# Splitting three of the seven products a second time in units 2 to 4 of an adjacency-attention kernel

## Chip, cores and metric

The kernel runs on one core of one Trainium2 chip. The metric is the device time of one execution in microseconds (us), the median over runs; lower is better. Engines are named as in the profile: PE (TensorE matmul), PEld (its weight loads), DVE (VectorE), ACT (ScalarE), POOL (GpSimd), SP (the queue that issues most loads).

## The reference, cut to what matters

x is 4096 x 512 and adj is 4096 x 4096, all float32. Two layers run after one another; the change touches only the last product of the second one.

```python
def _L1_gnn_ref(x, adj, weight, bias, node_w, edge_w):
    node_att = softmax(x @ node_w, axis=0)
    h = x @ edge_w
    e = h @ h.T
    e = where(adj > 0, e, NEG_BIG)
    edge_att = softmax(e, axis=1)
    combined_att = node_att * edge_att
    support = x @ weight
    output = adj * combined_att @ support
    return output + bias
...
x = layernorm(x + _L0_gnn_ref(x, adj, L0_gnn_weight))
x = layernorm(x + _L1_gnn_ref(x, adj, L1_gnn_weight, ...))
```

The kernel computes adj * combined_att times x first and multiplies by `weight` afterwards, row block by row block.

## The kernel before, in words

**Stages.** Up to about 870 us the first layer runs, then h is made, then the scores e with their row minima and sums are written to DRAM. From 1081.8 us to the end, the stage that matters here, the *aggregate*, multiplies the weights by x. It consists of 16 units, `blocks` (L1256), each an `Aggregate(g, r)`: g is one of four pairs of 512-wide column groups of the result (groups g and g+4), r one of four pairs of 512-deep blocks that are summed over. Units 1 to 4 are the first column pair (g = 0; r = 0, 1, 2, 3), units 5 to 8 the second, and so on. A unit's number n in the code is one less: `n` = 0 to 3 is the first pair.

**A unit.** It is a 2 x 2 block product done by seven products instead of eight. Its right operands are four square pieces of 512 x 512 weights, `self.q`, in buffers of 8 KB per partition, and three combinations `t2, t3, t4` of them; its left operands lie ready in DRAM, `lop_d[r][:, m]` for m = 0 to 6 (512 deep, 256 wide). While unit n is multiplied, the other engines make the right operands of unit n+1. `steps` (L858) lists this work with the fraction of the unit at which each item is traced: load scores and adjacency (POOL queue), `shift` (L823, DVE), `exp` and `clip` (L826 and L829, ACT), `weigh` (L835, DVE), `combine` (L848 to L856, DVE). There are twelve DVE operations of 128 x 2048 in it. `extra`, two more such buffers, is taken when n reaches 4.

**A product.** In the plain form product m is two objects `Sums(unit, m, h)`, h = 0 and 1, each with a PSUM bank of its own, four matmuls of 128x128 by 128x512. `in_two(n)` (L1258) says which units use the other form: there the products m in `SPLIT = 6, 4, 3` are themselves done by seven products of half size, in four `Sums` with `ns` = (1, 2), (6,), (0, 5), (3, 4), where `ns` are the numbers of the half-size products in that bank, each two matmuls of 128x128 by 128x256. `in_two` is true for n = 4 to 14: every column pair but the first, and not the last unit. `order` (L914) gives the order of the products; in a split unit it is one end, 6, 5, 4, 0, 3, the other end.

**What a split product needs.** Right combinations: `second` (L935; four DVE operations of 128 x 512, L942 to L946), written into `extra[0]` and over the old right operand. Left combinations: `lefts` (L949; four DVE operations of 128 x 256, L955 to L958, in the two `left2` buffers of the pool `rows`, which has four buffers). In this kernel the units of the first pair make them after each plain product m in `SPLIT` has been multiplied, from the left operand that lies in SBUF, and ACT sends them to DRAM (`lop2_d`, L962); the units of the other pairs read them back together with the raw quarters (L1048 to L1052).

**Sums over r.** A bank is copied by ACT to `sums` (or, for ns (0, 5) and (6,), to `extra`) when its product is done (`evict`, L1074) and copied back into a bank before the same product of the next unit (`seed`, L1037). When the fourth unit of a pair is done, the half-size products are put together by `join_inner` (L1098, seven DVE operations of 128 x 256 for each m, L1113), then the seven products by `join` (L1115, 128 x 1024, L1128). `Finish` (L1132) then multiplies by `weight` (L1192, PE) and adds into x (L1203, DVE). It runs off the list `todo` during the next three units.

**What sets the order.** The text of the program gives each engine's stream roughly; the framework's scheduler may move an instruction forward on its engine when it holds it ready. `tc.keep_in_program_order` pins an instruction behind the one traced before it on its engine. PE's products follow `plan`; `seed` runs up to three `Sums` ahead; left operands are loaded by SP into the pool `lopp` (four buffers).

Of the kernel before, what the change touches and what calls it, by code (L numbers as in the profile page):

```python
# [11 lines left out]
F32 = mybir.dt.float32  # L12
# [6 lines left out]
P = 128  # L19
# [4 lines left out]
SHIFT = 1.5 * 2.0**34  # L24
SPLIT = 6, 4, 3
WARM = 12


@with_exitstack
def kernel(  # L30
# [13 lines left out]
    nc = tc.nc  # L44
# [3 lines left out]
    W = 512  # L48
# [605 lines left out]
    class Couple:  # L654
# [9 lines left out]
        def operands(self):  # L664
            A, B, h = self.A, self.B, KD // 2
            if B not in Couple.right:
                r11, r12 = (hT[:, :h, ts(c, W)] for c in (B, B + 1))
                r21, r22 = (hT[:, h:, ts(c, W)] for c in (B, B + 1))
                t1, t2, t3, t4 = (lopp.tile([P, h, W], F32, name="right", tag="lop") for _ in range(4))
                nc.vector.tensor_sub(t1, r12, r11)  # L670
                nc.vector.tensor_sub(t2, r22, t1)
                nc.vector.tensor_sub(t3, r22, r12)
                nc.vector.tensor_sub(t4, r21, t2)
                Couple.right[B] = r11, r21, r22, t4, t1, t2, t3
            low, high = (hT[:, f : f + h, ts(A, W)].rearrange("p k (q u w) -> p k q u w", u=2, w=P) for f in (0, h))
            l11, l21 = (low[:, :, :, u, :] for u in range(2))
            l12, l22 = (high[:, :, :, u, :] for u in range(2))
            Couple.made[0] += 1
            self.sums = None
            if Couple.made[0] % 2:  # L680
                s2, s1, s3, s4 = (rows.tile([P, h, 2, P], F32, name="left", tag="rows") for _ in range(4))
            else:
                self.sums = Uses(1)
                s2, s1, s3, s4 = (
                    self.sums.buf[:, n, :].rearrange("p (k q w) -> p k q w", k=h, w=P) for n in range(4)
                )
            nc.vector.tensor_add(s1, l21, l22)
            nc.vector.tensor_sub(s2, s1, l11)
            nc.vector.tensor_sub(s3, l11, l21)
            nc.vector.tensor_sub(s4, l12, s2)  # L690
            self.left = l11, l12, s4, l22, s1, s2, s3
# [107 lines left out]
    class Aggregate:  # L799
# [2 lines left out]

        def __init__(self, g, r):
            self.g, self.r = g, r

        def load(self, n):
            r, c = self.r + n // 2 * HG, self.g + n % 2 * HG
# [138 lines left out]
            nc.vector.tensor_sub(t4, r21, t2)  # L946
            yield

        def lefts(self, m, lop):  # L949

            (l11, l21), (l12, l22) = [[lop[:, k : k + 2, f : f + P] for f in (0, P)] for k in (0, BG // 2)]
            s = [rows.tile([P, 2, BG // 2, P], F32, name="left2", tag="rows") for _ in range(2)]
            s4, s3, s2, s1 = (x[:, n] for x in s for n in range(2))

            tc.keep_in_program_order(nc.vector.tensor_add(s1, l21, l22))  # L955
            tc.keep_in_program_order(nc.vector.tensor_sub(s2, s1, l11))
            tc.keep_in_program_order(nc.vector.tensor_sub(s3, l11, l21))  # L957
            tc.keep_in_program_order(nc.vector.tensor_sub(s4, l12, s2))  # L958
            to = lop2_d[self.r][:, SPLIT.index(m)]
            yield  # L960
            for n in range(2):
                nc.scalar.dma_start(to[:, ts(n, 2)], s[n])  # L962
# [5 lines left out]
        def main(self, between, two):  # L968
            uses = deque(u for u in plan if u.unit is self)
            whole = sum(u.work for u in uses)  # L970
            halves = (None for m in [u.m for u in uses if u.ns and u.ns[0] == 1] for _ in self.second(m))
            stores = deque()
            past = 0
            while plan and plan[0].unit is self:
                u = plan.popleft()
                u.seed()
                u.multiply()
                evict()
                written.append(u)
                for ahead in list(plan)[:3]:  # L980
                    ahead.seed()
                past += u.work
                if stores:
                    next(stores.popleft(), None)
                if not u.ns:
                    next(halves, None)
                if u.end:
                    free.append(self.right(u.m))
                    if not self.g and u.m in SPLIT:
                        stores.append(self.lefts(u.m, lops["lop"]))  # L990
                        next(stores[0])
                between(past / whole, u.work)
            if stores:
                next(stores.popleft(), None)
# [4 lines left out]

        joins = {0: (0,), 5: (1,), 6: (2,), 4: (3, 4, 5), 3: (6,)}  # L1000

    lops = {}
    kept = deque()
    written = deque()

# [2 lines left out]
    class Sums:  # L1008
# [5 lines left out]
        def __init__(self, unit, m, h=0, more=False, keep=False, ns=None):  # L1014
            self.unit, self.m, self.h, self.more, self.keep, self.ns = unit, m, h, more, keep, ns
            self.work = 2 * len(ns) if ns else 8
            self.begin = ns[0] == 1 if ns else not h
            self.end = ns[0] == 3 if ns else bool(h)
            self.w = W // 2 * len(ns) if ns else W
            self.bank = None  # L1020

        def to(self):

# [2 lines left out]
        def seed(self):  # L1026


            if self.bank is not None or self.more and not kept:
                return  # L1030
            if self.more:
                self.bank = kept.popleft()
                return
            self.bank = banks.popleft()
            if self.unit.r:
                assert self.ns or not any(m == self.m for m, _ in [*inner, *inner_next])
                nc.scalar.copy(self.bank[:, : self.w], self.to())  # L1037
            elif self.w < W:
                nc.vector.memset(self.bank[:, : self.w], 0.0)

        def multiply(self):
            r, m = self.unit.r, self.m
            if self.begin and not self.ns:
                lops["lop"] = lopp.tile([P, BG, HD], F32, name="lop")
                nc.sync.dma_start(lops["lop"], lop_d[r][:, m])
            elif self.begin:
                low, high = (lopp.tile([P, 4, BG // 2, P], F32, name="lop2", tag="lop") for _ in range(2))
                raw, s = lop_d[r][:, m], lop2_d[r][:, SPLIT.index(m)]  # L1048
                nc.sync.dma_start(low[:, :2].rearrange("p n b f -> p (n b) f"), raw[:, :, :P])
                nc.sync.dma_start(low[:, 2:], s[:, :2])  # L1050
                nc.sync.dma_start(high[:, :2], s[:, 2:])
                nc.sync.dma_start(high[:, 2], raw[:, BG // 2 :, P:])  # L1052
                lops["low"], lops["high"] = low, high
            if self.ns:
                products = []
                for k, n in enumerate(self.ns):
                    at = self.lefts[n]
                    lop = lops["high"][:, at - 4] if at > 3 else lops["low"][:, at]
                    products.append((self.bank[:, ts(k, W // 2)], lop, self.unit.halves[n], BG // 2))
            else:  # L1060
                products = [(self.bank, lops["lop"][:, :, ts(self.h, P)], self.unit.right(m), BG)]
            start = not r and self.w == W
            for ps, lop, rop, K in products:
                for k in range(K):
                    nc.tensor.matmul(ps, lop[:, k, :], rop[:, k, :], start=start, stop=(k == K - 1), skip_group_check=True)  # L1065
                    start = False
            if self.keep:
                kept.append(self.bank)

        def evict(self):  # L1070
            u = self.unit
            if not self.keep:
                assert u.r or not self.ns or not any(m == self.m for m, _ in [*inner, *inner_next])
                nc.scalar.copy(self.to(), self.bank[:, : self.w])  # L1074
                banks.append(self.bank)
            if self.end and self.ns and (u.r == HG - 1 or blocks.index(u) == len(blocks) - 2):
                inner_next.extend((self.m, n) for n in range(7))
            if self.end and u.last:
                for done in u.joins.get(self.m, ()):
                    join(u.g, done, nc.vector)  # L1080
# [176 lines left out]

    def in_two(n):  # L1258

        return HG <= n < len(blocks) - 1  # L1260

    def couples(B, *As):
        return [Couple(A, B) for A in As]
# [82 lines left out]
    for n, u in enumerate(blocks):  # L1346
# [5 lines left out]
        if n == 0:  # L1352
            first.extend((0.05, f) for _, f in early_)
            first.extend((0.13 + n // 2 * 0.07, lambda n=n: u.combine(n)) for n in range(4))
        elif n == HG:
            extra.extend(take() for _ in range(2))
        if nxt:
            steps = nxt.steps()
# [81 lines left out]
```

## Time and profile before

| what | value |
|---|---|
| median of 3 runs | 1941.57 us (1939.22 to 1943.59) |
| span of the profiled execution | 1940.4 us, mean granted clock 0.999 |
| unit 1 (n = 0) | 1081.82 to 1131.83 us |
| unit 2 (n = 1) | 1131.83 to 1179.90 us |
| unit 3 (n = 2) | 1179.90 to 1227.97 us |
| unit 4 (n = 3) | 1227.97 to 1277.82 us |
| units 5 to 16 | 1277.82 to 1909 us |

The units' edges are the starts of their first aggregate matmul (line L1065) in the order of time. A float32 matmul of the program is two MATMUL rows in the trace (1094 are issued at L1065, 2188 rows are there); a row is called a *pass* below. A row's duration is longer than the distance to the next row, because passes overlap, so costs on PE are read as distances from start to start. In the answer by stretches, each line gives a stretch in us, its length, and for each engine the busy time with the number of instructions in brackets, then the granted clock, the share of the DMA engines and GB/s.

### The profile page before, as it was taken

To read this page: it belongs to the slowest core of one execution; us is meant where nothing else is said; L and a number is where in the kernel's file an instruction comes from. 1 tells how busy PE (TensorE), PEld (TensorE's weight loads), DVE (VectorE), ACT (ScalarE), POOL (GpSimd) and SP (SyncE) were. 2 spreads that over 40 slices of the span, in tenths; PEclk is the share of its full clock that TensorE was granted. 3 is DMA by queue.
4 is the path that set the end of the run, shared out by engine and by line. 5 is a ranking of instruction groups with operands and counts; after the bars stand their busy time and mean duration, and the time that the engine had idled before them with its cause. 6 is when DMAs were issued, how large, how long until landed. Compare 5 with 4: busy or idle time off the path is not lost.

```text
span 1940.4 us, 20257 instructions
## 1 busy us (share of the span) xinstructions
PE 1918.7 (99%) x6742; PEld 1203.0 (62%) x6742; DVE 1389.6 (72%) x2062; ACT 1022.4 (53%) x1614; POOL 299.5 (15%) x424
## 2 busy tenths in 40 slices
PE   9999999999999999999999999999999999999998
PEld 6888888888644445454555444456666666666655
DVE  7766676676774566567566796687879987798737
ACT  5433333333202567566667566546766576757731
POOL 0122222222341111011112111111111101111100
PEclk9999999999999999999999999999999999999999
DMA  9888888888475478577769998787778787887831
GB/s 311 296 325 310 293 324 308 323 306 293 147 274 213 166 253 320 183 279 254 274 249 336 330 336 296 259 284 248 260 268 290 262 278 254 294 274 265 274 108 44
DMA packets 171751, 517.11 MB, mean 267 GB/s; under 512 B 15872, under 2 KB 41216, under 8 KB 163968
## 3 DMA queue, kind: packets, MB, share of 16 engines
q1 hardware_dynamic: 89472, 226.39, 35.0%
q0 software_dynamic: 66912, 247.49, 34.2%
q10 hardware_dynamic: 15264, 41.95, 5.9%
q8 instruction: 53, 0.87, 0.2%
q14 instruction: 50, 0.41, 0.1%
HBM read 389.94 MB, written 125.83 MB: 266 GB/s over the span
## 4 chain that ended last, share of the span: by engine, by line
PE 76%; DVE 10%; issue 6%; DMA 6%; ACT 1%; POOL 1%; POOLq 0%; DVEq 0%; SPq 0%; ACTq 0%
PE bank L1065 25%; PE seven L702 12%; PE acc L374 11%; PE acc L373 11%; PE pe L633 4%; PE seven L101 4%; PE po L1192 3%; PE pt L603 2%; DMA s_d<-slot 2%; DMA slot<-s_d 2%; DVE lent L835 1%; PE acc L246 1%; PE pw L214 1%; PE pt L333 1%; DVE over L1128 1%
## 5 line engine op out<-in xcount | busy, mean ns | idle before, releaser
L1065 PE MATMUL bank<-lent,lop 128*128 128x512 f32 (+1 forms) x1292 | 424.6, 479 | 0.7 <-issue 0.7
L373 PE MATMUL acc<-xw,hi 128*128 128x512 f32 x960 | 376.4, 392 | 0.0
L374 PE MATMUL acc<-xw,lo 128*128 128x512 f32 x960 | 374.2, 390 | 0.0
L1065 PE MATMUL bank<-slot,lop 128*128 128x512 f32 (+1 forms) x896 | 347.0, 535 | 0.3 <-DVE slot L850 0.3
L1065 PEld LDWEIGHTS bank<-lent,lop 128*128 128x128 f32 x1292 | 245.2, 190 | 155.0 <-issue 133.6
L1065 PEld LDWEIGHTS bank<-slot,lop 128*128 128x128 f32 x896 | 170.0, 190 | 153.4 <-issue 142.3
L363 ACT CAST hi<-at 128x1024 fp32r<-128x1024 f32 x120 | 126.4, 1054 | 203.3 <-PE acc L373 148.4
L365 DVE TENSOR_TENSOR lo<-at,hi 128x1024 fp32r<-128x1024 f32 x120 | 146.9, 1224 | 85.3 <-ACT hi L363 85.3
L374 PEld LDWEIGHTS acc<-xw,lo 128*128 128x128 f32 x960 | 180.3, 188 | 37.0 <-DVE lo L365 0.3
L373 PEld LDWEIGHTS acc<-xw,hi 128*128 128x128 f32 x960 | 180.3, 188 | 36.7
L1074 ACT COPY over<-bank 128x512 f32<-128x512 f32 x200 | 114.9, 581 | 121.3 <-PE bank L1065 109.9
L633 PE MATMUL pe<-hT 128*128 128x512 f32 (+3 forms) x384 | 132.1, 486 | 0.0
L574 ACT ACTIVATE line<-line,nmax_c 128x512 f32<-128x512 f32 x160 | 114.8, 724 | 20.9 <-DVE nmax_c L565 20.8
L565 DVE CUSTOM_DVE_ANT_0 line<-lent,slot 128x512 f32<-128x512 bf16 x144 | 93.1, 689 | 45.2 <-ACT slot L643 22.4
L829 ACT ACTIVATE slot<-slot 128x2048 f32<-128x2048 f32 x40 | 76.5, 1913 | 73.8 <-DMA slot<-in_adj_t_dram 64.7
L823 DVE CUSTOM_DVE_ANT_1 slot<-slot,line 128x2048 f32<-128x2048 f32 x36 | 82.4, 2288 | 32.2 <-DMA slot<-s_d 31.7
L633 PEld LDWEIGHTS pe<-hT 128*128 128x128 f32 x384 | 64.6, 191 | 41.4 <-issue 33.8
L702 PE MATMUL seven<-hT 128*128 128x512 f32 x192 | 89.8, 593 | 0.0
L826 ACT ACTIVATE slot<-slot 128x2048 f32<-128x2048 f32 x36 | 68.9, 1913 | 33.5 <-DVE slot L823 32.5
L1037 ACT COPY bank<-over 128x512 f32<-128x512 f32 x144 | 84.8, 596 | 2.9 <-DVE left L957 0.2
L603 PEld LDWEIGHTS pt<-ident,lent 128*128 128x128 f32 x412 | 51.1, 141 | 55.1 <-issue 40.0
L604 ACT COPY slot<-pt 128x512 f32<-128x512 f32 (+3 forms) x126 | 69.5, 555 | 27.8 <-PE pt L603 24.0
(260 smaller groups left out, 2864.9 us busy)
## 6 DMA issues: line engine op xcount, KB each, us to landing
at<-in_adj_t_dram SPq DMA_DIRECT2D x60, 1024.0 KB, 6.9
slot<-in_adj_t_dram POOLq DMA_DIRECT2D x42, 1024.0 KB, 6.7
lop<-lop_d SPq DMA_DIRECT2D x79, 512.0 KB, 4.7
slot<-s_d POOLq DMA_DIRECT2D x36, 1024.0 KB, 7.5
s_d<-slot POOLq DMA_DIRECT2D x33, 1024.0 KB, 6.9
lent<-s_d POOLq DMA_DIRECT2D x28, 1024.0 KB, 7.9
lop<-lop_d SPq DMA_DIRECT2D x99, 256.0 KB, 4.4
lent<-in_adj_dram SPq DMA_DIRECT2D x48, 512.0 KB, 4.9
```

The costliest lines, as they stand in the source:

```text
L363: nc.scalar.copy(hi, aq)
L365: nc.vector.tensor_sub(lo, aq, hi.bitcast(F32))
L373: nc.tensor.matmul(acc, hi[:, c, :], xw[:, kb, :], start=(kb == 0), stop=False)
L374: nc.tensor.matmul(acc, lo[:, c, :], xw[:, kb, :], start=False, stop=(kb == NB - 1))
L565: nc.vector.tensor_tensor_reduce(line, mask, src, -1.0, HUGE, ALU.add, ALU.min, accum_out=nmax_c[:, b, c : c + 1])
L574: nc.scalar.activation(line, line, AF.Exp, bias=nmax_c[:, b, c : c + 1], scale=-1.0, accum_out=sum_c[:, b, c : c + 1])
L603: nc.tensor.transpose(pt[:, j, :], src[:, ts(j, P)], ident)
L633: nc.tensor.matmul(pe[:, lo * P :], hT[:, k, ts(A * BG + i, P)], hT[:, k, (B * BG + lo) * P : (B + 1) * W], start=(k == 0), stop=(k == KD ...
L702: nc.tensor.matmul(ps, left[m][:, k, q, :], right[m][:, k, :], start=(first and k == 0), stop=(k == KD // 2 - 1), skip_group_check=not first,)
L1037: nc.scalar.copy(self.bank[:, : self.w], self.to())
L1065: nc.tensor.matmul(ps, lop[:, k, :], rop[:, k, :], start=start, stop=(k == K - 1), skip_group_check=True)
L1074: nc.scalar.copy(self.to(), self.bank[:, : self.w])
```

## The change

`in_two` becomes true from n = 1. So products 6, 4 and 3 are split in units 2, 3 and 4 too. The purpose is to have seven half-size products there instead of eight.

In these units a split product doesn't read its left combinations from DRAM: `operands` loads the raw left operand whole, `combine` calls `lefts` up to two `Sums` ahead, and the matmuls read the `left2` buffers and the raw quarters in SBUF. ACT still sends the combinations to DRAM, after the product, for the other column pairs. In all units, the loads of left operands are now traced up to `AHEAD` = 2 `Sums` ahead.

Unit 1 stays plain. Its result for a split m is laid into two of the half-size sums: the half-size sums (1, 2) and (3, 4) of unit 2 are seeded from it, after one DVE subtraction of 128 x 256 for each m, and (0, 5) and (6,) start fresh in unit 2 (a bank that is only half used is zeroed by DVE, L1039). `extra` is taken at n = 1 instead of n = 4. Since the first pair now has half-size sums, `join_inner` runs for it as well, during unit 4.

```diff
+AHEAD = 2
...
-        def lefts(self, m, lop):
+        def lefts(self, m):
+            lop = self.whole[m]
...
+            self.split[m] = l11, l12, s4, l22, s1, s2, s3
...
                 u.seed()
+                u.operands()
+                for ahead in list(plan)[:AHEAD]:
+                    ahead.operands()
                 u.multiply()
...
                     if not self.g and u.m in SPLIT:
-                        stores.append(self.lefts(u.m, lops["lop"]))
-                        next(stores[0])
+                        u.combine()
+                        stores.append(self.stores[u.m])
+                for ahead in list(plan)[:2]:
+                    if ahead.ns and ahead.begin and not self.g:
+                        ahead.combine()
...
+            self.fresh = not unit.r or unit is blocks[1] and ns in ((0, 5), (6,))
...
-            if self.unit.r:
+            if not self.fresh:
...
+        def operands(self):
+
+            u, m = self.unit, self.m
+            if not self.begin or m in u.whole or m in u.split:
+                return
+            raw = lop_d[u.r][:, m]
+            if not self.ns or not u.g:
+                u.whole[m] = lopp.tile([P, BG, HD], F32, name="lop")
+                nc.sync.dma_start(u.whole[m], raw)
+                return
...
+        def combine(self):
+
+            u, m = self.unit, self.m
+            if m not in u.stores:
+                u.stores[m] = u.lefts(m)
+                next(u.stores[m])
...
-            start = not r and self.w == W
+            start = self.fresh and self.w == W
...
+                if u is blocks[0] and self.end and self.m in SPLIT:
+                    upper, lower = (sums[:, 0, self.m, h, W // 2 :] for h in range(2))
+                    nc.vector.tensor_sub(upper, upper, lower)
...
-        return HG <= n < len(blocks) - 1
+        return 0 < n < len(blocks) - 1
...
-        elif n == HG:
+        elif n == 1:
             extra.extend(take() for _ in range(2))
```

## The prediction

> **What bounds the kernel now.** I read the page's first part, then the PE rows in order of time at the end of unit 8, then busy time by stretch with one stretch per unit, then the waits of PE and DVE. The page:
>
> ```profile
> PE 1918.7 (99%) x6742; PEld 1203.0 (62%) x6742; DVE 1389.6 (72%) x2062; ACT 1022.4 (53%) x1614; POOL 299.5 (15%) x424
> ```
>
> PE is the bound of the whole, if its busy time can be trusted. The Trainium skill ("Perfetto Trace Analysis", section "Identifying the Most-Contended Engine") says matmul busy share is a poor measure, since pipelined passes look different from what they cost. This trace agrees: plain passes of L1065 are listed at a mean of 592 ns but start 429 ns apart. So I price by starts. The PE rows in order of time (start, length, line, passes):
>
> ```profile
> 1467.94 7.03 PE L1065 MATMUL bank<-slot,lop 128*128 128x512 f32 x16
> 1474.81 6.21 PE L1065 MATMUL bank<-lent,lop 128*128 128x256 f32 x28
> 1480.85 7.03 PE L1065 MATMUL bank<-slot,lop 128*128 128x512 f32 x16
> 1487.72 1.45 PE L1065 MATMUL bank<-lent,lop 128*128 128x512 f32 x3
> ```
>
> These are a plain product, a split product (14 matmuls, 28 passes), a plain product, and the next unit. Plain: 1487.72 - 1480.85 = 6.87 us for 16 passes, 0.429 each. Split: 1480.85 - 1474.81 = 6.04 us for 28 passes, 0.216 each. Both forms stand side by side here, without a gap. Now the stretches (length, then PE, PEld, DVE, ACT, POOL busy); the first seven lines are units 1 to 5, 8 and 9:
>
> ```profile
> 1081.82:1131.83 50.01, 48.90 (x115) 21.10 (x114) 46.77 (x44) 32.43 (x45) 8.97 (x12) 1.00 0.95 349
> 1131.83:1179.90 48.07, 48.07 (x113) 21.28 (x112) 39.61 (x29) 30.25 (x33) 6.00 (x8) 1.00 0.90 330
> 1179.90:1227.97 48.07, 48.07 (x114) 21.28 (x113) 24.65 (x22) 25.14 (x31) 5.98 (x8) 1.00 0.82 284
> 1227.97:1277.82 49.85, 49.85 (x129) 23.07 (x128) 43.51 (x41) 28.65 (x35) 5.24 (x7) 1.00 0.75 252
> 1277.82:1329.46 51.64, 51.64 (x177) 33.44 (x176) 42.27 (x46) 26.66 (x31) 5.24 (x7) 1.00 0.73 256
> ...
> 1440.33:1487.72 47.39, 47.39 (x166) 29.91 (x165) 38.87 (x43) 34.30 (x48) 5.98 (x8) 1.00 0.82 288
> 1487.72:1539.28 51.56, 51.04 (x173) 32.59 (x172) 51.43 (x53) 27.93 (x32) 6.72 (x9) 1.00 0.77 265
> ```
>
> Units 2 and 3 last 48.07 = 112 x 0.429: nothing but plain passes, no gap. Unit 4 has 16 short passes of L772 more (1.8 us). Unit 8 is the split form of the same place in the next column pair, with the same 16 passes and nothing of Finish: 47.39 against 49.85. So the split pays 2.46 us a unit where it runs already, with no PE idle time, while DVE has 38.87 busy of 47.39. In unit 9 DVE is busy 51.43 of 51.56, and PE still loses only 0.5. The waits of DVE in units 2 to 4 (in all us, times, longest):
>
> ```profile
> DVE nm L763 <- PE bank L772: 17.5, 1, 17.5
> DVE lent L835 <- ACT slot L829: 6.3, 1, 6.3
> DVE slot L823 <- DMA slot<-s_d: 5.5, 2, 5.2
> DVE slot L835 <- ACT lent L829: 4.0, 2, 3.5
> ```
>
> and the only wait of PE in units 5 to 12 (1277.82 to 1699.17):
>
> ```profile
> PE po L1192 <- DVE xb L1203: 3.3, 5, 1.3
> ```
>
> PE has no wait at all in units 2 to 4. DVE is ahead of it there, by up to 17.5 us; that is the room the change must live in. In split units PE never waits for a combination, only for Finish's DVE work (L1203).
>
> **The skill on what is concerned.** "TensorE: Matmul & The Clock Gate", the table at its head: TensorE's queue pulls weight loads ahead of running matmuls, the other engines are strict first-in first-out. The trace agrees on both: a half-size pass has its own weight load of 190 ns, yet passes start 216 apart, so the load is hidden (26 ns to spare); and DVE stood 17.5 us behind one reduction. "VectorE: DVE Perf Modes", section "Walkthrough: the 8-slice pipeline in each mode": float32 tensor_tensor yields one result per cycle, at 0.96 GHz, so 256, 512 and 2048 elements take 0.27, 0.53 and 2.13 us (estimate from that page). The rows in order of time give 0.34, 0.60 and 2.20 from start to start, which is the page's figure plus 0.07; I use the measured ones.
>
> ```profile
> 1259.05 0.42 DVE L957 TENSOR_TENSOR left<-lop 128x256 f32<-128x256 f32 x1
> 1259.39 0.42 DVE L958 TENSOR_TENSOR left<-lop,left 128x256 f32<-128x256 f32 x1
> 1259.72 2.28 DVE L850 TENSOR_TENSOR slot<-slot,lent 128x2048 f32<-128x2048 f32 x1
> 1261.93 0.69 DVE L942 TENSOR_TENSOR lent<-lent 128x512 f32<-128x512 f32 x1
> 1262.53 2.28 DVE L853 TENSOR_TENSOR lent<-slot,slot 128x2048 f32<-128x2048 f32 x1
> ```
>
> **The change part by part.**
>
> *PE.* Nine products (three in each of three units) go from 16 x 0.429 = 6.87 to 28 x 0.216 = 6.05, which is -0.82 each, **-7.4 us** in all (three times the 2.46 seen between units 4 and 8). All of it is on the path, since PE has no wait there.
>
> *DVE, right combinations.* 9 x 4 x 0.60 = 21.6 us added in units 2 to 4. *Inner joins:* 21 x 0.34 = 7.1 us; unit 8 shows 16 of 21 inside its own stretch, so 5.4 in unit 4 and 1.7 in unit 5. *Zeroing of half banks in unit 2:* 3 x 0.27 (L1039 in unit 4's stretch) = 0.8. *Three subtractions in unit 1:* 3 x 0.34 = 1.0. Left combinations: the same twelve sets of 4 x 0.34, only moved ahead of the product. Moved out of unit 4: four outer joins (L1128, 4.9 us), as they wait until the inner ones are done. Units 2 to 4 then ask DVE for 39.6 + 24.7 + 43.5 + 21.6 + 5.4 + 0.8 - 4.9 = 130.7 us, of 146.0 - 7.4 = 138.6: 94%. That is above unit 8 (82%), below unit 9 (99.7%). It lies beside PE, so I cost its bulk at nothing; what hides it is 138.6 us of passes.
>
> *The new wait.* A split product's second half-size product reads s4, the last of a pinned chain of four (4 x 0.34 = 1.36 us), which waits for the raw operand's load (4.7 us median to landing) and for whatever DVE runs before it. The chain is traced two `Sums` ahead, so PE then has two plain `Sums` (6.9 us) or two split ones (3.5 us) in hand; between two split products there is always a plain one, so 6.9 holds. Queued behind the chain on DVE are shift, weigh and combine for the next unit, due only at its end, and for these ACT's exp. Ahead of it can stand one or two 2.2 us operations: 1.36 + 2.4 (right combinations) + 2.2 = 6.0 of 6.9 us with one, 8.2 with two. So the exposed time is nought to 1.3 a product. The same margin is met today by the right combinations of split units without one PE wait, so I take nought for eight products, and 0.4 for the first in unit 2, where DVE comes from a full unit 1 (46.77 busy of 50.01) with the three subtractions on top.
>
> *Loads and buffers.* The raw operand is loaded whole, as before: no bytes more. `lopp` has four buffers and a plain or raw operand takes one, so SP issues it some three products (20 us) early: hidden. `AHEAD` therefore changes nothing that I can see. Two of thirteen buffers leave the pool at n = 1; units 5 to 15 run with eleven and no PE wait outside L1192: nothing. Seeds and evictions rise to what unit 8 shows, ACT 34.3 of 47.4: beside PE.
>
> *Units 5 to 7.* They take over joins: DVE 42.27 + 4.9 + 1.7 = 48.9 of 51.6, which is unit 9's picture. Units 9 to 11 have 559 PE instructions, as units 5 to 7 have, and last 51.56 + 56.85 + 55.65 = 164.06 against 51.64 + 59.23 + 51.64 = 162.51. So up to **+1.5 us**, at L1192. I take 1.5; the low end is 0 or a little less, as units 13 to 15 show fewer such gaps.
>
> *Sum.* -7.4 + 0.4 + 1.5 = -5.5: 1941.6 - 5.5 = 1936.1 us.
>
> **The rivals.**
>
> *A (forecast).* PE stays the bound and keeps all but 1 to 3 us of the 7.4: 1936.1, between 1934 and 1938. For it: unit 8 against unit 4; no wait of PE on combinations in eleven split units. Against: those units made no left combinations.
>
> *B: DVE eats the gain.* At 94% with in-order waits, every lag behind ACT (6.3 and 4.0 us in the waits above) comes out on PE once DVE no longer has its lead. If half a chain is exposed at each of nine products, 9 x 0.68 = 6.1: -7.4 + 1.5 + 6.1 = +0.2, so 1941.8. For it: the lead of 17.5 us is used up by 21.6 us of new work. Against: unit 9 at 99.7% loses 0.5 us.
>
> *C: the left combinations become the bound.* If the whole chain is exposed at each split product, 9 x 1.36 = 12.2: 1941.6 - 7.4 + 1.5 + 12.2 = 1947.9, slower. With a 2.2 us operation ahead as well it is 9 x 3.56 = 32 us: 1967.7. For it: the chain is pinned, so it can't be moved ahead of a waiting instruction. Against: 6.9 us of PE work in hand.
>
> **How the numbers follow.** A 0.70, B 0.18, C 0.12. Predicted is A's 1936.1. The low end is the full 7.4 with no loss, 1934.2, less about a microsecond of the runs' scatter (they lie 2.4 below and 2.0 above their median): 1933.0. The high end takes in B with some scatter: 1942.8; C is left out. Faster by over 0.2% means below 1937.7: nearly all of A and a little of B, 0.70. Within 0.2% (to 1945.5): B and the edge of A, 0.19. Slower: C, 0.11.
>
> **What would show it.** Right: units 2 and 3 last about 45.6 us, unit 4 about 47.4, PE busy for all of each; 684 + 240 half-size passes grow by 252; DVE is about 94% busy in units 2 to 4 and its 17.5 us wait is mostly gone; units 5 to 7 last 163 to 164 us with the loss at L1192. Wrong in the way of B or C: waits of PE at L1065 for `left2` (L958), for L942 to L946, or for seeds behind a late ACT, in units 2 to 4. A PE wait for a load of `lop`, or unit 2 starting late because of the subtractions in unit 1, would break the steps that I costed at nothing.

## The result and the profile after

| | median | range of the runs |
|---|---|---|
| before | 1942.58 us | 1939.22 to 1944.55 |
| after | 1950.30 us | 1946.14 to 1956.63 |

The ratio is 1.0042, with a 95% interval of 1.0025 to 1.0059: slower by about 8 us, where 5.5 us less were forecast. The profiled execution of after has a span of 1945.3 us against 1940.4. It is the second fastest of the six runs, so the trace holds 4.9 us of the loss; the other 3 us or so are in no trace. (One slip in the description of the stages above: in the trace the h stage starts at 507 us and the scores at 606 us; the first layer is over by then, not at 870. Nothing in the argument rests on it.)

In the changed kernel the line numbers differ: the aggregate matmul is L1088 (L1065 before), the Finish matmul L1218 (L1192), its addition on DVE L1229 (L1203), the eviction L1097 (L1074), the seed L1047 (L1037); shift, weigh and combine are L825, L837 and L850 to L858, exp and clip L828 and L831, the left combinations L958 to L961. The first part of the page of after:

```profile
PE 1914.4 (98%) x6850; PEld 1224.2 (63%) x6850; DVE 1419.8 (73%) x2125; ACT 1032.4 (53%) x1644; POOL 299.6 (15%) x424
```

There are 108 more passes (252 half-size ones added, 144 plain ones gone), and PE is busy 4.3 us less, while the span is 4.9 us longer. PE has thus become idle for longer. Busy time by stretch says where; the lines are units 2 to 8 of after:

```profile
1130.61:1176.20 45.59, 45.59 (x149) 28.12 (x148) 41.12 (x41) 31.29 (x40) 6.00 (x8) 1.00 0.88 318
1176.20:1225.22 49.02, 46.13 (x149) 27.95 (x148) 42.26 (x42) 32.53 (x44) 5.97 (x8) 1.00 0.82 300
1225.22:1272.61 47.39, 47.39 (x166) 29.91 (x165) 39.00 (x51) 30.08 (x44) 5.98 (x8) 1.00 0.83 287
1272.61:1327.13 54.52, 51.04 (x174) 32.59 (x173) 53.73 (x56) 29.91 (x35) 6.38 (x9) 1.00 0.74 262
1327.13:1390.80 63.67, 58.22 (x198) 38.13 (x196) 50.54 (x63) 43.88 (x56) 7.08 (x10) 0.97 0.78 262
1390.80:1445.03 54.23, 54.23 (x190) 35.72 (x188) 37.73 (x51) 36.41 (x50) 4.49 (x6) 1.00 0.72 250
1445.03:1492.41 47.38, 47.38 (x165) 29.91 (x164) 38.94 (x44) 34.21 (x48) 5.99 (x8) 1.00 0.82 290
```

| stretch | before | after | difference |
|---|---|---|---|
| up to the end of unit 1 | 1131.8 | 1130.6 | -1.2 |
| units 2 to 4 | 146.0 | 142.0 | -4.0 |
| units 5 to 7 | 162.5 | 172.4 | +9.9 |
| unit 8 to the end | 500.0 | 500.3 | +0.3 |

Units 2 and 4 are what the passes promised, to a tenth of a microsecond: 45.59 and 47.39. Unit 3 lost 3.4 us. Units 5 to 7, whose own passes the change doesn't touch, lost 9.9. The waits of PE in units 2 to 4, in all us, times, longest:

```profile
PE bank L1088 <- ACT bank L1047: 1.6, 1, 1.6
PE bank L1088 <- DVE left L961: 1.3, 1, 1.3
```

and in units 5 to 7:

```profile
PE po L1218 <- DVE xb L1229: 8.9, 3, 3.5
```

These three waits hold most of it: 8.9 us, where the same units before had one wait of 1.3 us. After one of them the granted clock of PE falls to half for 3.4 us, and the slow passes add another 1.7 us (last section). A Finish matmul adds into the PSUM half that DVE's addition L1229 must have read first; the addition is short (0.48 us), so what counts is what stands ahead of it in DVE's stream. The DVE rows of after in order of time, at each of the three waits:

```profile
1307.71 2.28 DVE L837 TENSOR_TENSOR slot<-slot,lent 128x2048 f32<-128x2048 f32 x1
1309.92 2.28 DVE L837 TENSOR_TENSOR lent<-lent,slot 128x2048 f32<-128x2048 f32 x1
1312.12 0.18 DVE L790 TENSOR_TENSOR d<-d,sum_c 128x32 f32<-128x32 f32 x1
1312.24 2.29 DVE L850 TENSOR_TENSOR slot<-lent,lent 128x2048 f32<-128x2048 f32 x1
1314.44 0.48 DVE L1229 SCALAR_TENSOR_TENSOR xb<-po,f,xb 128x256 f32<-128x256 f32 x1
...
1350.04 2.29 DVE L825 CUSTOM_DVE_ANT_1 slot<-slot,line 128x2048 f32<-128x2048 f32 x1 [0.40 <-DMA slot<-s_d]
1352.25 0.48 DVE L1229 SCALAR_TENSOR_TENSOR xb<-po,f,xb 128x256 f32<-128x256 f32 x1
...
1387.09 2.29 DVE L825 CUSTOM_DVE_ANT_1 lent<-lent,line 128x2048 f32<-128x2048 f32 x1 [4.13 <-DMA lent<-s_d]
1389.30 0.48 DVE L1229 SCALAR_TENSOR_TENSOR xb<-po,f,xb 128x256 f32<-128x256 f32 x1
```

At the first, a combination for the *next* unit (L850) stands ahead of the addition. At the other two it is a shift (L825) for the next unit, and at the last that shift itself stood 4.13 us until its load had landed. None of these is due before the end of the unit; the addition is due at once.

### The profile page after: what moved, and what is told of

It is laid out like the page before. It is cut to its first block, busy times and chain, and to the rows that moved or that the text cites. A ratio compares the mean times of both kernels' runs of the same rounds, so it can differ in the third digit from the quotient of the medians.

```text
span 1945.3 us, 20584 instructions
## 1 busy us (share of the span) xinstructions
PE 1914.4 (98%) x6850; PEld 1224.2 (63%) x6850; DVE 1419.8 (73%) x2125; ACT 1032.4 (53%) x1644; POOL 299.6 (15%) x424
## 4 chain that ended last, share of the span: by engine, by line
PE 68%; DVE 12%; DMA 8%; issue 8%; ACT 3%; POOL 1%; POOLq 0%; ACTq 0%; DVEq 0%; SPq 0%
PE bank L1088 16%; PE seven L703 13%; PE acc L375 11%; PE acc L374 11%; PE pe L634 4%; PE seven L102 4%; PE po L1218 3%; DMA slot<-in_adj_t_dram 3%; PE pt L604 2%; DMA slot<-s_d 1%; DVE lent L837 1%; DMA lent<-in_adj_t_dram 1%; DMA lent<-s_d 1%; DVE lent L825 1%; ACT line L575 1%
## 5 line engine op out<-in xcount | busy, mean ns | idle before, releaser
L1088 PE MATMUL bank<-lent,lop 128*128 128x256 f32 (+1 forms) x1264 | 405.1, 470 | 2.0 <-ACT bank L1047 1.6
L1088 PE MATMUL bank<-slot,lop 128*128 128x512 f32 (+1 forms) x888 | 334.2, 521 | 0.3 <-DVE slot L852 0.3
L1088 PEld LDWEIGHTS bank<-lent,lop 128*128 128x128 f32 x1264 | 241.0, 191 | 140.3 <-issue 115.5
L1088 PEld LDWEIGHTS bank<-slot,lop 128*128 128x128 f32 x888 | 168.4, 190 | 137.4 <-issue 125.3
L1097 ACT COPY over<-bank 128x512 f32<-128x512 f32 x200 | 114.5, 581 | 98.7 <-PE bank L1088 91.8
L831 ACT ACTIVATE slot<-slot 128x2048 f32<-128x2048 f32 x43 | 82.2, 1912 | 103.2 <-DMA slot<-in_adj_t_dram 90.7
L825 DVE CUSTOM_DVE_ANT_1 slot<-slot,line 128x2048 f32<-128x2048 f32 x36 | 82.3, 2287 | 32.2 <-DMA slot<-s_d 32.2
L1047 ACT COPY bank<-over 128x512 f32<-128x512 f32 x144 | 85.1, 597 | 2.7 <-ACT over L1097 0.2
L828 ACT ACTIVATE slot<-slot 128x2048 f32<-128x2048 f32 x36 | 69.0, 1916 | 22.9 <-DVE slot L825 22.8
```

What stands on the lines that cost most here:

```text
L825: pinned[0](nc.vector._custom_dve(TENSOR_ADD_SAT, out=q, in0=q, in1=m, s0=0.0, s1=-HUGE))
```

## Theories

1. **Amount.** The added DVE work (combinations, inner joins) makes DVE late, and units 5 to 7 pay.
2. **Order.** DVE has time enough over the stage; what costs is that urgent short additions stand behind long operations that aren't urgent, at places the scheduler chose.
3. **Loads.** Left operands traced earlier, or two buffers fewer from unit 2 on, delay other transfers.

## Experiments

Each is an edit of the changed kernel; units are as above. All ratios are to the kernel before.

**e1_frame: the rewritten code without the early split.**

```diff
-        return 0 < n < len(blocks) - 1
+        return 4 <= n < len(blocks) - 1
-        elif n == 1:
+        elif n == 4:
```

(and the first pair's `fresh` and subtraction left off, which then apply to nothing)

> The rewritten operand code of the change (loads traced two Sums ahead, left combinations through `combine`), but the split starts with unit 5 as before and the two extra buffers are taken there. Theory 1 (DVE falls behind in unit 4 because of the added combinations and inner joins, and PE then waits in units 5 to 7 for Finish's additions): same as before, 1942.6 within 2 us, units 5 to 7 together about 162.5 us. Theory 2 (the earlier loads of left operands disturb the slot loads): 1947 or more, units 5 to 7 about 168 to 172.

Measured: 1943.06 us, ratio 0.9997 (0.9988 to 1.0005); units 5 to 7 162.2 us. The new code for operands and the earlier loads cost nothing. So the first half of theory 3 is ruled out.

**e2_from4th: only unit 4 split.** The same edit with 3 for 4, and `fresh` and the subtraction moved to units 4 and 3.

> Only unit 4 is split in the first pair; units 2 and 3 stay plain, the extra buffers are taken at unit 4. Theory 1 in its narrow form (what counts is the DVE work in and after unit 4: its left combinations and the inner joins): units 5 to 7 still near 172 us against 162.5, and the total 1942.6 - 2.5 + 9 = about 1949. Rival (the lag is built up over units 2 to 4, or the buffers taken early are missing): units 5 to 7 at 163 to 166, total about 1942.

Measured: 1951.68 us, ratio 1.0041 (1.0026 to 1.0056). Units 5 to 7 take 174.0 us, and PE waits there on the additions (passes at half clock after these waits add some 5 us):

```profile
PE po L1218 <- DVE xb L1229: 7.2, 3, 3.7
```

So about two thirds of the gain were given up and all of the loss kept. The loss needs no lag built up over units 2 and 3 and no buffers taken two units earlier: what happens in unit 4 and after it is enough.

**e3_nojoin: no inner joins for the first pair.**

```diff
-            if self.end and self.ns and (u.r == HG - 1 or ...):
+            if self.end and self.ns and u.g and (u.r == HG - 1 or ...):
```

> The change, with the inner joins of the first column pair left out (21 DVE operations of 128 x 256, 7 us; the outer joins read the sums unjoined, so the first pair's result is not the reference's). Theory 1: units 5 to 7 fall from 172.4 to about 164 us and the total to about 1942. Rival (late slot loads, whatever DVE does): units 5 to 7 stay over 170.

Measured: 1943.73 us, ratio 1.0001 (0.9993 to 1.0010); units 5 to 7 164.2 us. That fits theory 1, and it was my reading at this point. But taking the joins out also moves everything behind them in DVE's stream, so it does not tell amount from order.

**e4_slow: the Finish of the first pair handed out more slowly.**

```diff
-            while owed[0] >= 6:
-                owed[0] -= 6
+            pace = 8 if u.g == 1 else 6
+            while owed[0] >= pace:
+                owed[0] -= pace
```

> The change, with the items of the Finish of the first pair handed out every 8 units of PE work instead of every 6, so that it spreads over units 5 to 8. Theory 1 (DVE has too much to do in units 5 and 6 and too little in 7 and 8): units 5 to 8 together fall from 219.8 to about 212 us, total about 1941. Rival (the wait of each Finish product on its addition is the same wherever it lies): units 5 to 8 stay at 218 to 220, total about 1950.

Measured: 1946.62 us, ratio 1.0018 (1.0008 to 1.0028). Units 5 to 8 take 214.9 us instead of 219.8, less of a fall than expected, and units 9 to 11 take 169.1 instead of 164.1, in the profiled execution (the slowest of its runs, at 1951.93 us). Units 5 to 7 are down to 163.2, but unit 8 takes 51.7 instead of 47.4. Spreading the work helped where it was thinned and cost where it was put.

**e5_pin: shifts and large combinations of units 5 to 7 kept in program order on DVE.** No work is removed or added.

```diff
-        pinned[0] = tc.keep_in_program_order if n == 0 else lambda ins: ins
+        pinned[0] = tc.keep_in_program_order if n in (0, 4, 5, 6) else lambda ins: ins
```

> The change, with the shifts and the large combinations of units 5 to 7 pinned to their place in the program's order on DVE, as they are in unit 1. If what counts is that the scheduler has put shifts that wait for a load ahead of Finish's additions (DVE order), units 5 to 7 fall from 172.4 to about 165 us and the total to about 1944. If what counts is the amount of DVE work, they stay at 170 or more, total about 1950.

Measured: 1940.11 us, ratio 0.9985 (0.9977 to 0.9994): faster than before. Units 5 to 7 fall from 172.4 to 163.8 us. The place of the first wait, DVE rows of e5_pin:

```profile
1310.51 2.28 DVE L837 TENSOR_TENSOR lent<-lent,slot 128x2048 f32<-128x2048 f32 x1
1312.71 0.18 DVE L790 TENSOR_TENSOR d<-d,sum_c 128x32 f32<-128x32 f32 x1
1312.81 1.07 DVE L1229 SCALAR_TENSOR_TENSOR xb<-po,f,xb 128x256 f32<-128x256 f32 x2
1313.80 2.28 DVE L850 TENSOR_TENSOR slot<-lent,lent 128x2048 f32<-128x2048 f32 x1
```

The two additions now stand ahead of L850. So L850 had been moved ahead of its place in the program. With the same DVE work, 8.6 of the 9.9 us are back (the slow passes among them): the order costs, and the amount alone does not.

**e6_leftsact: left combinations as ACT copies.**

```diff
-            tc.keep_in_program_order(nc.vector.tensor_add(s1, l21, l22))
+            nc.scalar.copy(s1, l21)
...
```

(all four, with l11, l21, l12 as sources; the combinations themselves are left out, so the split products are not those of the reference)

> The change, with the four DVE operations of each set of left combinations replaced by four ACT copies of the same size (the combinations are then raw quarters, so the results of the split products are not the reference's). It takes 4.1 us of DVE work out of each of units 1 to 4 and puts about 4.7 us on ACT. Theory 1 (amount of DVE work up to the start of unit 5): the waits of unit 3 go (48 to 49 down to about 46 us), units 5 to 7 fall from 172.4 to about 167, total about 1943. Rival (only the inner joins count): units 5 to 7 stay at 171 to 173, total about 1948.

Measured: 1960.11 us, ratio 1.0091 (1.0075 to 1.0106). This run is only half of a test: the copies were free to move, the first of them runs at 1015.7 us, in the score stage, and unit 1 begins at 1090.8 us instead of 1081. (10.2 us at half clock from 1017.0 us on are a part of that delay.) Units 5 to 7 take 175.2 us with less work on DVE, which speaks against theory 1. e11_actpin repeats it without the flaw.

**e7_both: ACT copies and no inner joins** (both edits together).

> Left combinations as ACT copies and no inner joins for the first pair (both change the result, as said for each alone): all DVE work that the change adds is gone but the right combinations. Theory 1: units 2 to 4 take their 138.6 us of passes, units 5 to 7 are near the 162.5 of before, total about 1936 to 1938, which is what the passes alone promise. Rival (buffers or loads bind as well): units 5 to 7 stay at 166 or more, total 1941 or more.

Measured: 1953.27 us, ratio 1.0056 (1.0041 to 1.0071). It shares the flaw (unit 1 begins at 1088.5 us). Of the 10.3 us over the before run beside it, some 7 are that late start, and units 5 to 7 still take 168.4 us with PE waiting 5.1 us for L1229. Over units 1 to 7 DVE is busy 288.8 us, against 311.1 in the change and 280.8 before. So three quarters of the added DVE time can be gone, and more than half of the waits remain.

**e8_two: products 6 and 4 alone.**

```diff
-                if two and m in SPLIT:
+                if two and m in SPLIT and (self.g or m != 3):
```

(and no subtraction for product 3)

> The change for products 6 and 4 alone; product 3 stays plain in the first pair. PE gains 4.9 instead of 7.3 us, and DVE has 2.4 us less of right combinations in each of units 2 to 4 and 2.4 us less of inner joins. Theory 1 with a threshold (a saturated DVE stream gives back more than it got): units 5 to 7 about 166 us, total about 1942. Rival (loss in proportion to the added work): units 5 to 7 about 169, units 2 to 4 about 143, total about 1948.

Measured: 1944.12 us, ratio 1.0006 (0.9994 to 1.0017); units 2 to 4 144.2 us, units 5 to 7 166.9 us. By its numbers it lies near the form of theory 1 with a threshold. But it is again another order on DVE, and by then e5_pin had shown how much that does; it settles nothing alone.

**e9_pin2to7: the pin in units 1 to 7** (`n <= 6`).

> The change with shifts and large combinations pinned to program order in units 1 to 7, so in the newly split units too. If the order on DVE is what costs time there as well, the two waits of unit 3 (3.4 us) go, units 2 to 4 together take 139 to 140 us instead of 142 to 143, units 5 to 7 about 164, total 1937 to 1938. If the waits of unit 3 come from something else (ACT's seeds, late loads), units 2 to 4 stay at 142 or more and the total at 1940 or above.

Measured: 1940.11 us, ratio 0.9985 (0.9978 to 0.9992). Busy time by stretch, units 3 and 5 to 7:

```profile
1177.73:1228.54 50.81, 48.09 (x149) 28.93 (x148) 42.67 (x43) 34.86 (x50) 5.97 (x8) 0.97 0.81 294
...
1275.93:1326.70 50.77, 50.77 (x173) 32.68 (x172) 50.50 (x53) 26.03 (x31) 6.38 (x9) 1.00 0.77 271
1326.70:1382.66 55.96, 55.96 (x198) 37.24 (x196) 48.09 (x61) 43.33 (x55) 6.19 (x9) 1.00 0.79 276
1382.66:1436.89 54.23, 54.23 (x190) 35.72 (x188) 40.44 (x53) 37.12 (x50) 5.38 (x8) 1.00 0.77 271
```

Units 5 to 7 take 161.0 us, less than before the change, and PE has no wait in them, although DVE is busy 50.50 of 50.77 in unit 5. A DVE at 99% cost PE nothing in this order. Unit 3 got no better (50.8 us, with waits of 2.7 us and 3.4 us at half clock after them), so its waits have another cause.

**e10_framepin: the pin of units 5 to 7 without the early split.**

> The rewritten operand code with the split from unit 5 on, as before, and the pin of units 5 to 7 alone. If the pin only undoes what the change did to DVE's order, it brings nothing here: 1942.5 to 1943, units 5 to 7 at 161 to 163. If the pin is a gain of its own, 1940 or less.

Measured: 1941.57 us, ratio 0.9994 (0.9987 to 1.0000); units 5 to 7 161.4 us. That lies between the two cases: a small gain of its own, by the median 1.5 us, as the one wait of unit 6 before (1.3 us) goes too. Most of e5_pin's 10 us against the change is repair.

**e11_actpin: e6 with each copy pinned on ACT.**

> As the run with left combinations as ACT copies (raw quarters in their place, so the split products are not the reference's), but each copy pinned to its place in ACT's program order, so that none moves into the stage before and unit 1 starts at 1081 us again. Amount of DVE work in units 1 to 4 is 16 us less than in the change. If that amount sets the loss, units 5 to 7 take about 166 us and the total is about 1942. If the order of DVE's instructions in units 5 to 7 sets it, they stay at 171 or more and the total at about 1950.

Measured: 1948.87 us, ratio 1.0026 (1.0015 to 1.0037). Unit 1 begins at 1083.5 us, so the flaw is mostly gone. Units 2 to 5:

```profile
1133.40:1180.83 47.43, 45.86 (x149) 28.00 (x148) 37.62 (x29) 35.05 (x52) 5.98 (x8) 1.00 0.85 305
1180.83:1231.13 50.30, 46.87 (x149) 27.71 (x148) 35.02 (x26) 35.39 (x55) 5.98 (x8) 1.00 0.79 277
1231.13:1278.52 47.39, 47.39 (x166) 29.91 (x165) 34.70 (x37) 33.93 (x53) 6.00 (x8) 1.00 0.79 282
1278.52:1335.92 57.40, 53.67 (x173) 34.45 (x172) 57.24 (x62) 29.22 (x35) 6.39 (x9) 0.94 0.71 248
```

In units 2 to 4 DVE is busy 107.3 us, 15.1 less than in the change (41.12 + 42.26 + 39.00 = 122.4), and yet units 5 to 7 take 169.8 us; DVE is busy 34.70 of 47.39 us in unit 4 and 57.24 of 57.40 in unit 5, so the freed time didn't reach the place of the loss. Theory 1 had 166 and order 171 or more, so the time is nearer to order; but 6.8 us in unit 5 are at half clock, which adds some 3 us, and PE's waits fell from 8.9 to 5.0 us. This run alone doesn't decide. e5_pin and e9_pin2to7 do, where the work stayed and the loss went.

**e12_pinall: the pin in every unit.**

> The change with shifts and large combinations pinned in every unit. If the order on DVE is also what makes PE wait in units 9 to 15 (about 4 us there), the total falls to about 1935. If those waits are short enough already, or program order is worse there than the scheduler's, it is 1938 to 1942.

Measured: 1936.11 us, ratio 0.9961 (0.9951 to 0.9970). Units 9 to 11 fall from 164.1 to 161.0. Unit 3 alone takes 51.5 us: PE waits 1.7 us for a seed and 1.9 us for a left combination, and passes at half clock follow. The same two waits are in after. The ACT rows of after at the first, where PE needed a seed at 1189.1 (e12_pinall has the same rows in the same order):

```profile
1183.45 1.92 ACT L828 ACTIVATE lent<-lent 128x2048 f32<-128x2048 f32 x1 [6.24 <-DVE lent L825]
1185.65 1.91 ACT L828 ACTIVATE lent<-lent 128x2048 f32<-128x2048 f32 x1 [0.29 <-DVE lent L825]
1187.47 0.57 ACT L1097 COPY over<-bank 128x512 f32<-128x512 f32 x1
1187.94 1.91 ACT L831 ACTIVATE slot<-slot 128x2048 f32<-128x2048 f32 x1
1189.75 0.57 ACT L1097 COPY over<-bank 128x512 f32<-128x512 f32 x1
1190.21 1.12 ACT L1047 COPY bank<-over 128x512 f32<-128x512 f32 x2
```

The eviction and the seeds stand behind two exps and a clip, and the first exp stood 6.24 us until DVE's shift was done. It is the same fault on another engine. At the second wait PE needed the last left combination (L961) at about 1211.6; the DVE rows of after:

```profile
1205.38 2.29 DVE L837 TENSOR_TENSOR slot<-slot,slot 128x2048 f32<-128x2048 f32 x1 [1.98 <-ACT slot L828]
...
1208.19 2.28 DVE L850 TENSOR_TENSOR slot<-slot,lent 128x2048 f32<-128x2048 f32 x1
...
1212.60 0.42 DVE L961 TENSOR_TENSOR left<-lop,left 128x256 f32<-128x256 f32 x1
```

DVE had itself waited for ACT, and a large combination and the right combinations stand ahead of the left ones.

**e13_early: left combinations up to four `Sums` ahead** (with the pin in every unit).

```diff
-                for ahead in list(plan)[:AHEAD]:
+                for ahead in list(plan)[: AHEAD if self.g else 4]:
...
-                for ahead in list(plan)[:2]:
-                    if ahead.ns and ahead.begin and not self.g:
+                for ahead in list(plan)[:4]:
+                    if not ahead.unit.g and ahead.ns and ahead.begin and not self.g:
```

> The change with the pin in every unit, and the left combinations of the first pair made up to four Sums ahead instead of two, so ahead of the right combinations and of a large combination on DVE. If the second wait of unit 3 is their place in DVE's order, it goes: unit 3 takes about 47.5 us instead of 51.5, total about 1933. If the second wait only moves elsewhere (DVE late because of ACT and loads), unit 3 stays at 49 or more and the total at about 1936.

Measured: 1934.72 us, ratio 0.9963 (0.9949 to 0.9977). PE no longer waits for the left combinations, but for seeds (1.8 us) and right combinations (2.4 us), now partly in unit 2. Unit 3 takes 47.9 us, as the first case said, but unit 2 takes 48.5 instead of 45.6; units 2 to 4 are 143.8 us. So the place of the left combinations in DVE's order was the cause of the second wait, but most of the time was lost again elsewhere.

**e14_actorder: exp and clip pinned on ACT** (with the pin in every unit).

```diff
-            nc.scalar.activation(self.q[n], self.q[n], AF.Exp)
+            pinned[0](nc.scalar.activation(self.q[n], self.q[n], AF.Exp))
```

(and the same for clip)

> The change with the pin in every unit, and exp and clip pinned to program order on ACT as well, so that they can't be moved ahead of seeds traced before them. If the first wait of unit 3 is ACT's order, it goes (unit 3 about 49.5 us, total about 1934). If the seeds stand behind exp in program order too, nothing changes in unit 3 and the total is 1936 or, where program order is worse on ACT, more.

Measured: 1936.07 us, ratio 0.9968 (0.9958 to 0.9979). Both waits of unit 3 are gone from their places; one of 1.8 us is new, for a seed behind a clip that stood 4.5 us until its load had landed (unit 3 48.3 us). But unit 1 takes 54.7 us instead of 50: there, program order on ACT is worse than the scheduler's. PE waits 3.1 us in it, and 6.8 us at half clock follow, where 16 passes take 9.73 us instead of 7.03.

**e15_both: e13 and e14 together.**

> Both. If unit 3's two waits have these two causes, units 2 to 4 take about 139 us and the total is about 1932. If the slot loads bind behind them, units 2 to 4 stay above 141 us.

Measured: 1932.73 us, ratio 0.9952 (0.9937 to 0.9966). Units 2 to 4:

```profile
1136.23:1181.83 45.60, 45.60 (x149) 28.14 (x148) 43.55 (x43) 30.89 (x40) 6.00 (x8) 1.00 0.89 328
1181.83:1227.43 45.60, 45.60 (x150) 28.16 (x149) 36.53 (x36) 31.05 (x42) 5.99 (x8) 1.00 0.80 283
1227.43:1274.81 47.38, 47.38 (x165) 29.94 (x164) 44.34 (x54) 33.22 (x47) 6.00 (x8) 1.00 0.86 309
```

They take 138.6 us in all, exactly their passes, with eleven buffers and every added operation in place. So the second half of theory 3 falls too. Unit 1 still pays (55.7 us), and that gives DVE and ACT more time before unit 2, which the next run takes away.

**e16_order: as e15, but unit 1 without the pin on ACT**, and beside it **e17_frameorder: the same order without the early split.**

```diff
+        held[0] = tc.keep_in_program_order if n else lambda ins: ins
...
-            nc.scalar.activation(self.q[n], self.q[n], AF.Exp)
+            held[0](nc.scalar.activation(self.q[n], self.q[n], AF.Exp))
```

> The change with shift and combinations pinned on DVE in every unit, left combinations of the first pair up to four Sums ahead, and exp and clip pinned on ACT in every unit but the first. If the 5.7 us lost in unit 1 came from that pin, unit 1 takes 50 us again, units 2 to 4 138.6, total about 1927 to 1929. If units 2 to 4 were clean only because unit 1 gave DVE time to get ahead, they go back above 141 and the total stays at 1931 or more.

> The same order on DVE and ACT, with the split from unit 5 on as before. If the split of units 2 to 4 is worth its passes (7.4 us) once the order is right, this is 7 us above the run beside it, at 1934 to 1936: units 2 to 4 146.0, units 5 to 7 160 to 161. If the order alone brings what the run beside it brings, both are within 2 us of each other.

Measured: e16_order 1931.85 us, ratio 0.9936 (0.9924 to 0.9949); e17_frameorder 1936.80 us, ratio 0.9971 (0.9962 to 0.9981). Unit 1 of e16_order takes 50.5 us again. Units 2 to 4 take 139.7, with one wait of 0.5 us left, so a part of e15's cleanness did come from the slow unit 1; the total of e16_order is 3 us above what I expected. In the profiled execution its unit 1 also begins late, at 1084.0 us against 1081.4 in e12_pinall. In its score stage the clock is at 0.50 from 1037.9 to 1041.4 us, and eight passes take 4.70 us there instead of 3.60; that is 1.1 us, and the rest stays open. Units 2 to 4 of e17_frameorder take 146.0. The split itself is thus worth 6.3 us in these stretches and 5.0 by the medians, once both kernels have the same order. e16_order is the fastest kernel of the study, 0.6% ahead of the one before; about half of that is the split and half the order.

## Why the prediction was wrong, point by point

- **PE's term (-7.4 us): right.** Units 2 and 4 last 45.59 and 47.39, as forecast, and e15_both shows all three at their passes. The prices of 0.429 and 0.216 us, and the hidden weight load, held. One remark beside them needs a correction: the Trainium skill ("Perfetto Trace Analysis", section "Identifying the Most-Contended Engine") says that pipelined matmuls look smaller in a trace, while here a row looks larger (592 ns) than its cost (429 ns). That busy time isn't the cost holds either way.
- **"The new wait", nought for eight products and 0.4 for unit 2: wrong in place and size.** Unit 2 was clean, unit 3 lost 3.4 us. The argument was that the chain of left combinations has 6.9 us in which to run. It left out that DVE itself may be late when the chain's turn comes: in unit 3 it had waited 2.0 us for ACT and had a large combination (L850) and the right combinations ahead of the chain.
- **"Seeds and evictions ... beside PE": wrong.** ACT was busy 32.5 of 49.0 us in unit 3, so by amount nothing stood in the way, but the seeds stood behind an exp that waited for DVE. That made a wait of 1.6 us on PE.
- **Units 5 to 7, "up to +1.5 us": the step that failed.** It measured +9.9 us. I took units 9 to 11 as the picture, since they have the same joins, the same number of passes and a DVE as full. They do have the same *amount* of work (DVE 138.8 us in units 9 to 11 before, 139.0 in units 5 to 7 of e9_pin2to7). What PE lost in them depended on the order that DVE happened to have there: e12_pinall takes units 9 to 11 from 164.1 to 161.0 us with the same work. The new stretch got another order: three additions behind operations that nobody needed yet, 7.6 us more of waits and 1.7 us at half clock. e9_pin2to7 has the same DVE work, 99% busy in unit 5, and no wait of PE.
- **DVE's bulk, "at nothing": right in amount, not in place.** Over units 1 to 7 DVE is busy 30.3 us more than before, and 30.5 had been worked out. But units 2 to 4 hold 122.4 us (86%) instead of 130.7, and units 5 to 7 hold 15.8 us more than before instead of 6.6: part of the work came later than worked out, where Finish's additions are. In e9_pin2to7 it is 12.8 us more in units 5 to 7, and PE has no wait there.
- **The rivals.** B and C looked for the loss inside units 2 to 4, at the split products, by lag or by the left chain. C had the sign and came near the size (1947.9) by luck, as the left chain cost only one wait of 1.3 us in after. What the prediction's own views showed and I used too little: the only PE wait of units 5 to 12 was L1192 on L1203. That was the one place where DVE's order already reached PE, and the change pushed more DVE work in front of it.
- **The stated signs.** "The loss at L1192" was named as the sign of the forecast, and it is there, only over six times as large. Two signs of B or C, a wait for a left combination and one for a seed behind a late ACT, came as well, 2.9 us in all in unit 3.

## What to carry to other kernels

When an engine works through its instructions in a fixed order, as DVE and ACT do in these traces, a free share of its time says little about what one more operation on it costs: ask which short operation another engine waits for, and what stands, or may be moved, ahead of it. Adding work can change the order that the scheduler lays down, even beyond the edited stages. A picture from another stage with the same amounts isn't a price, and pinning long, not urgent operations to program order is a cheap test, which here turned a loss of 0.4% into a gain of 0.4% (e12_pinall), though pinning on ACT in unit 1 cost 5 us (e14_actorder).

## What the runs showed of the hardware

One thing was not expected. After the second of the three waits in after (2.26 us, in unit 6), PE runs slowly for a while. Busy time by stretch, with the granted clock as the third figure from the end:

```profile
1353.00:1354.00 1.00, 1.00 (x6) 0.87 (x6) 0.06 (x1) 1.00 (x2) 0.00 (x0) 1.00 1.00 357
1354.00:1357.60 3.60, 3.60 (x11) 2.83 (x10) 2.37 (x2) 2.90 (x5) 0.00 (x0) 0.53 0.72 278
1357.60:1361.00 3.40, 3.40 (x17) 2.88 (x16) 3.40 (x5) 3.26 (x5) 0.75 (x1) 0.99 0.41 95
```

Eight half-size passes start some 0.43 us apart instead of 0.216, which costs another 1.7 us. The Trainium skill ("TensorE: Matmul & The Clock Gate", section "What's actually happening") describes a clock that halves after an idle window of about 3.4 us; here the half clock lasts about that long, but the wait ahead of it was shorter than the window. It doesn't follow every wait: the one of 3.48 us in unit 5 had no slow passes after it. In e16_order it came after waits of only 0.76 and 1.40 us, close together in the score stage.

In the clock records of all nineteen traces, every stretch at half clock before the last unit lasts 3.41, 6.83 or 10.24 us, that is one, two or three times 3.41. Such stretches add 1.7 us to the wait of 2.26 us here, and some 5 us to PE's waits of 7.2 in units 5 to 7 of e2_from4th: about 0.7 of the waits' length each time. So part of what a run pays or wins is not in the list of its waits. Whether this makes the runs of the kernel after scatter by 10 us (5 before) stays open: the mean clocks of its six runs, 0.996 to 0.998, do not follow their times.
